# Causal linear attention: values as the stationary operand, four heads in four quarters of columns, divisors from a block of ones

## The chip, the cores and the metric

The kernel runs on one core of a Trainium2 chip. The metric is the device time of one execution in microseconds (us). Three runs of the kernel before took 4279.67, 4286.88 and 4288.96 us; the median is 4286.88 us.

A core has four engines that compute, each with its own queue of instructions that it works off in order: TensorE (PE in the profile; its weight loads are PEld), VectorE (DVE), ScalarE (ACT) and GpSimd (POOL). SyncE (SP) issues the transfers (DMA). TensorE reads its operands from SBUF and writes results to PSUM; VectorE and ScalarE carry results from PSUM to SBUF.

## The reference

The input is 16 sequences of 256 tokens with 128 features. Four layers follow one another, each with a residual and a layer norm: linear attention with four heads, a mixture of eight experts, causal linear attention with 16 heads, and a block of six layers of windowed attention and feed-forward. The change is in the third of them. Cut to what matters:

```python
q = _heads(x @ Wq); k = _heads(x @ Wk); v = _heads(x @ Wv)   # 16 heads of 64
qf = _feature_map(q, Kq)      # softmax(f) and softmax(-f): 128 features
kf = _feature_map(k, Kk)
kv = jnp.cumsum(kf[:, :, :, None, :] * v[..., None], axis=2)
o = jnp.einsum('bhlf,bhldf->bhld', qf, kv)
z = jnp.einsum('bhlf,bhlf->bhl', qf, jnp.cumsum(kf, axis=2)) + EPS
o = o / z[..., None]
y = o.transpose(0, 2, 1, 3).reshape(x.shape[0], x.shape[1], H * HD)
return y @ Wo
```

So for every head and token, the values of all earlier tokens are summed with weights (the inner product of the query's and the key's features), and divided by the sum of those weights.

## The kernel before, in words

**Two stages.** The first holds linear attention (`linear`), experts (`experts`) and causal attention (`causal`); the second holds the six layers. Each stage has a list of steps. A step (class `Step`) belongs to one engine and issues a few instructions; it carries an expected cost in us, the steps it must follow, the buffers it takes, and a rank. `Plan.run` plays these steps through at their expected costs and always issues, on each engine, the ready step of the lowest rank whose buffers are free. The order in which it issues them is the order of the engine's queue on the chip. A wrong cost doesn't make a result wrong; it makes the order fit something else than the chip does. Ranks are offset by the two tables `due` (lines 371 to 399).

**Units.** The first stage works on eight units of two sequences each, that is four tiles of 128 tokens. For each unit `causal` (L761) transposes the stream, calls `part` (L803) four times (two sequences, two halves of eight heads), then `output` (L940) for every tile of 128 tokens, and normalizes.

**In `part`.** Values are computed token-major for eight heads (L817) and copied by ScalarE into the buffer `va` (L820), where each head has 64 columns and a 65th that is always 1.0 (it is set once, L445). Queries and keys go through the feature map: product (L829), largest and smallest of each head (L838, L839), differences on GpSimd (L842, L843), exp on ScalarE (L846), sums and reciprocals on VectorE (L850, L851), a division on GpSimd (L855), a clamp on VectorE (L858), transposes on TensorE (L874), a copy by ScalarE into `fT` (L880). Then come two groups of four heads. For each head:

- `scores` (L893, L894): keys' features times queries' features give the weights in one PSUM bank, with the key tokens as partitions: block 0 is tile 0 against itself, block 1 is keys of tile 0 against queries of tile 1, block 2 is tile 1 against itself.
- `diagonal` (L900, VectorE) masks blocks 0 and 2 with a triangle on the way into the buffer `A`; `below_it` (L906, ScalarE) copies block 1.
- `weigh` (L910 to L912): three matmuls with a block of `A` as the stationary operand and the 65 columns of `va` as the moving one. The result is token-major: 64 weighted sums, and in the 65th column the divisor. It lands in the buffer `two` (tile `pw`, two PSUM banks), of which there is one.

After the four heads `ratio` (L926, L927, L929, VectorE) adds 1e-12 to the divisors, takes their reciprocals, and multiplies the sums by them on the way into `y`, which is token-major and has one buffer per stage.

**In `output`.** Eight transposes of `y` (L951), two copies by ScalarE into `yT` (L954), eight matmuls with `W.o` that add up over the heads' features (L961), and an addition to the stream (L967).

**Weights.** SyncE issues all loads from one queue. `W.o` comes in one transfer (L429), with the heads' features in their natural order over eight blocks of 128 partitions.

Of the kernel before, what the change touches and what calls it, by code (L numbers as in the profile page):

```python
# [16 lines left out]
P = 128  # L17
# [182 lines left out]
def tile_kernel(ctx: ExitStack, tc: tile.TileContext, a: dict, out: bass.AP):  # L200
# [147 lines left out]
    with ExitStack() as st:  # L348
# [5 lines left out]
        def several(pl, n, shape, name):  # L354
# [7 lines left out]
            "h": several(wa, 4, [P, 384], "b_h"),  # L362
            "x": several(wa, 5, [P, 512], "bc_x"),
            "e": several(wa, 4, [P, 8, 2, DH], "c_e"),
            "va": several(wa, 3, [P, TPS, 8, DH + 1], "c_va"),
            "fT": several(wa, 10, [P, 4, SEQ], "c_fT"),
            "y": several(wa, 1, [P, TPS, HEADS, DH], "c_y"),
            "yT": several(wa, 1, [P, 8, P], "c_yT"),
            "A": several(wa, 4, [P, 3, P], "c_A"),
        }  # L370
        plan = Plan(slots, {
            "part.turn": 1.5,
# [29 lines left out]
        def keep_in(shape, src, name):  # L402
            return load(wa, shape, src, name)
# [22 lines left out]

        def weights_c():
            W.v = keep_in([P, INNER], a["L1_attn_Wv"], "c_wv")
            W.o = keep_in([P, 8, P], a["L1_attn_Wo"].rearrange("(c p) d -> p c d", p=P), "c_wo")  # L429
            W.tri = keep_in([P, 3 * P], a["c_tri"], "c_tri")  # L430

        def weights_d():
# [9 lines left out]
        wlb = step("sp", 6.0, weights_b, [wla], rank=-97)  # L442
        wlc = step("sp", 4.0, weights_c, [wlb], rank=-95)
        W.f = {nm: wa.tile([P, INNER], F32, name=f"c_wf{nm}", tag=f"c_wf{nm}") for nm in "qk"}
        for va in slots["va"]:  # L445
            pool.memset(va[:, :, :, DH : DH + 1], 1.0)

        def at(u, j):

# [311 lines left out]
        def causal(u, after, ready, done):  # L761
            rank = 4 * u + due["causal"]
            px, xT, r4 = Buf("bank"), Buf("x"), Buf("x")

            def turn():
                for j in range(TPU):
                    pe.transpose(px.t[:, j * P : (j + 1) * P], at(u, j), ident)

            tn = step("pe", 0.5, turn, [after], [px], [], rank, count=8)
            xc = copied(xT, None, px, 512, [tn], [xT], [], rank, 0.59)  # L770
            ends = []
            for s in range(SPU):
                y = Buf("y")
                ys = []
                for hh in range(2):
                    part(u, s, hh, rank + 2 * s + hh, xT, xc, ready, done, y, ys)
                for t in range(TPS):
                    ends.append(output(u, s, t, rank + 2 * s + 1.5, y, ys, r4, ends))
            nm = norm(
                "c", lambda j: r4.t[:, j * P : (j + 1) * P],  # L780
                lambda j: r4.t[:, j * P : (j + 1) * P], ends, [], [r4], rank + 4,
            )

            def save():
                sp.dma_start(out=keep[u], in_=r4.t)
# [12 lines left out]
            pz = Buf("bank")  # L798
            step("sp", 2.0, save, [nm], [], [r4], rank + 4)
            fn = step("pe", 0.5, partial(final, pz), [nm], [pz], [r4], rank + 4, count=8)  # L800
            step("act", 1.2, partial(stream, pz), [fn], [], [pz], rank + 4)

        def part(u, s, hh, rank, xT, xc, ready, done, y, ys):  # L803
# [8 lines left out]
            for t in range(TPS):  # L812
# [4 lines left out]
                    pe.matmul(pv.t, lhsT=xT.t[:, xj], rhs=W.v[:, c5], start=True, stop=True)  # L817

                def put_v(pv=pv, t=t):
                    act.copy(va.t[:, t, :, 0:DH], pv.t.rearrange("p (h d) -> p h d", d=DH))  # L820

                vm = step("pe", 0.9, values, [xc, wlc, gate, *vs], [pv] + ([] if t else [va]), [xT], rank + due["values"], count=4)
                vs.append(step("act", 0.6, put_v, [vm], [], [pv, va], rank))
# [59 lines left out]
                        fs_done[g].append(step("act", 0.6, put_f, [tn], [], [pz, f], rank))  # L883
            for g in range(2):
                po = Buf("two")
                last, pre = None, None
                for k in range(4):
                    pA, A = Buf("bank"), Buf("A")
                    hl = 4 * g + k

                    def scores(pA=pA, g=g, k=k):
                        qf, kf = fT["q", g].t[:, k, :], fT["k", g].t[:, k, :]
                        pe.matmul(pA.t[:, 0:SEQ], lhsT=kf[:, 0:P], rhs=qf, start=True, stop=True)  # L893
                        pe.matmul(  # L894
                            pA.t[:, SEQ : SEQ + P], lhsT=kf[:, P:SEQ], rhs=qf[:, P:SEQ],
                            start=True, stop=True,
                        )

                    def diagonal(pA=pA, A=A):
                        dve.tensor_tensor(  # L900
                            A.t[:, 0::2, :], pA.t[:, : 3 * P].rearrange("p (b n) -> p b n", n=P)[:, 0::2, :],
                            W.tri.rearrange("p (b n) -> p b n", n=P)[:, 0::2, :], ALU.mult,
                        )

                    def below_it(pA=pA, A=A):
                        act.copy(A.t[:, 1, :], pA.t[:, P : 2 * P])  # L906

                    def weigh(A=A, po=po, k=k, hl=hl):
                        c = slice(k * (DH + 1), (k + 1) * (DH + 1))
                        pe.matmul(po.t[:, 0, c], lhsT=A.t[:, 0, :], rhs=va.t[:, 0, hl, :], start=True, stop=True)  # L910
                        pe.matmul(po.t[:, 1, c], lhsT=A.t[:, 1, :], rhs=va.t[:, 0, hl, :], start=True, stop=False)
                        pe.matmul(po.t[:, 1, c], lhsT=A.t[:, 2, :], rhs=va.t[:, 1, hl, :], start=False, stop=True)  # L912

                    sc = step("pe", 0.66, scores, [*fs_done[g], pre], [pA, A], [fT["q", g], fT["k", g]], rank + due["scores"], count=8)
                    dg = step("dve", 0.45, diagonal, [sc], [], [pA, A], rank + due["diagonal"])
                    bl = step("act", 0.35, below_it, [sc], [], [pA, A], rank + due["diagonal"])
                    last = step(
                        "pe", 0.7, weigh, [dg, bl, *vs, last], [] if k else [po], [A, va] + ([po] if k else []),
                        rank + due["weigh"], count=12,
                    )  # L920
                    pre = sc

                def ratio(po=po, g=g):
                    o4 = po.t[:, :, : 4 * (DH + 1)].rearrange("p t (k d) -> p t k d", d=DH + 1)
                    z = sa.tile([P, TPS, 4], F32, name="c_z")
                    dve.tensor_scalar(z, o4[:, :, :, DH], FEPS, None, ALU.add)  # L926
                    dve.reciprocal(z, z)  # L927
                    h0 = 8 * hh + 4 * g
                    dve.tensor_tensor(  # L929
                        y.t[:, :, h0 : h0 + 4, :], o4[:, :, :, 0:DH], bc(z, [P, TPS, 4, DH], 3),  # L930
                        ALU.mult,
                    )

                first = not ys
                ys.append(
                    step("dve", 1.05, ratio, [last, *ys], [y] if first else [], [po] + ([] if first else [y]), rank + due["ratio"])
                )
            done.append(ys[-1])

        def output(u, s, t, rank, y, ys, r4, ends):  # L940
            j = s * TPS + t
            yT, pr = Buf("yT"), Buf("bank")
            cs = []
            for hf in range(2):
                pz = Buf("bank")

                def turn(pz=pz, hf=hf):
                    yt = y.t[:, t, :, :].rearrange("p h d -> p (h d)")
                    for k in range(4):
                        c = 4 * hf + k  # L950
                        pe.transpose(pz.t[:, k * P : (k + 1) * P], yt[:, c * P : (c + 1) * P], ident)  # L951

                def put(pz=pz, hf=hf):
                    act.copy(yT.t[:, 4 * hf : 4 * hf + 4, :].rearrange("p c n -> p (c n)"), pz.t)  # L954

                tn = step("pe", 0.5, turn, [*ys, *cs], [pz] + ([] if hf else [yT]), [y], rank + due["y"], count=8)
                cs.append(step("act", 0.6, put, [tn], [], [pz, yT], rank))

            def product():
                for c in range(8):  # L960
                    pe.matmul(  # L961
                        pr.t[:, :P], lhsT=yT.t[:, c, :], rhs=W.o[:, c, :],
                        start=(c == 0), stop=(c == 7),
                    )

            def add():
                dve.tensor_tensor(r4.t[:, j * P : (j + 1) * P], pr.t[:, :P], at(u, j), ALU.add)  # L967

            pm = step("pe", 1.86, product, cs, [pr], [yT], rank + due["y"], count=32)
            return step("dve", 0.3, add, [pm, *ends[-1:]], [] if ends else [r4], [pr] + ([r4] if ends else []), rank)  # L970

        ready = [*fused("q"), *fused("k")]
# [703 lines left out]
```

## Time and profile before

| | us |
|---|---|
| median of three runs | 4286.88 (4279.67 to 4288.96) |
| the profiled execution's own time | 4283.78 |
| its span, first to last instruction | 4281.5 |
| PE busy, whole span | 4026.8 (94%) |
| DVE busy, whole span | 3540.7 (83%) |
| ACT busy, whole span | 3147.6 (74%) |
| POOL busy, whole span | 2692.0 (63%) |
| last causal result stored (end of the first stage) | about 1097 |

How to read the lines that follow. A line of the groups names the source line, the engine, the operation, what it writes and reads, the shape and the count; after the bar stand the busy time in us, the mean duration of one instruction in ns, and the time that the engine sat idle just before these instructions, with what ended the idleness. A matmul of 32-bit numbers leaves two records (a transpose one), and records on PE overlap: what a matmul costs in a busy stretch is the distance from its start to the start of the next. `128*128` on PE is the part of the array that is used, rows by columns, so `64*32` is a tile of 64 rows and 32 columns. Lines of the timeline give start and duration in us and the number of records. Lines of stretches give busy time of each engine with the number of its instructions, the granted clock of PE, and the transfers' share. In the waits, "A <- B: 17.9, 9, 3.4" says that A's engine sat idle for 17.9 us in all, nine times, at most 3.4 us, until B was done.

### The profile page before, as it was taken

Reading aid. Unit: us, or ns where it says so; the run is one execution under the profiler, and the core shown is the slowest. Engines: PE = TensorE matmul, PEld = TensorE weight load, DVE = VectorE, ACT = ScalarE, POOL = GpSimd, SP = SyncE. Lnnn points to the kernel's source line nnn. Section 1 sums busy time; section 2 is a strip of 40 time slices with the busy share of each in tenths; the row PEclk is TensorE's granted clock in tenths of the full one; section 3 lists DMA queues with packets and bytes.
Section 4 is the critical chain, followed back from the end, with each engine's and each line's share of the span. In section 5 each row is a group of like instructions: output and inputs, shape, how many; then the busy total and the mean of one; then the engine's idle time right before and its main releaser. Section 6 shows DMA issues by size and latency. Waiting matters only on the chain.

```text
span 4281.5 us, 104658 instructions
## 1 busy us (share of the span) xinstructions
PE 4026.8 (94%) x43728; PEld 2666.5 (62%) x43728; DVE 3540.7 (83%) x5201; ACT 3147.6 (74%) x6106; POOL 2692.0 (63%) x2865
## 2 busy tenths in 40 slices
PE   8999999999799999999999999999999999999888
PEld 5777777787455555565565565565555565555555
DVE  6888888787688888888888888888888888888886
ACT  6766766665478778787778777778787787777675
POOL 2654555566676676667666666766666666766662
PEclk9999999999899999999999999999999999999999
DMA  3000000000000000000000000000000000000000
GB/s 89 4 6 6 4 1 4 3 4 3 20 2 11 2 13 2 7 12 2 13 2 7 11 2 13 2 7 12 2 13 2 7 12 2 2 2 4 9 7 25
DMA packets 30836, 37.03 MB, mean 9 GB/s; under 512 B 5406, under 2 KB 24348, under 8 KB 29596
## 3 DMA queue, kind: packets, MB, share of 16 engines
q1 hardware_dynamic: 30364, 30.35, 2.4%
q8 instruction: 343, 5.62, 0.6%
q14 instruction: 129, 1.06, 0.1%
HBM read 26.15 MB, written 4.19 MB: 7 GB/s over the span
## 4 chain that ended last, share of the span: by engine, by line
PE 54%; DVE 25%; POOL 9%; ACT 8%; issue 4%; SPq 0%; DMA 0%; ACTq 0%; POOLq 0%; DVEq 0%
PE pp L1086 10%; PE pp L1341 8%; PE pp L1160 6%; DVE d_t L1093 5%; DVE d_t L1100 5%; PE pp L1402 4%; ACT d_sq L1107 4%; PE pp L1293 4%; DVE d_e L1242 3%; POOL d_e L1279 3%; PE pp L1234 3%; POOL d_t L1110 2%; PE pp L1422 2%; PE pb L665 2%; DVE d_eT L1283 2%
## 5 line engine op out<-in xcount | busy, mean ns | idle before, releaser
L1110 POOL TENSOR_TENSOR d_t<-d_t,d_t 128x1024 f32<-128x1024 f32 x384 | 904.4, 2360 | 770.0 <-DVE d_t L1093 734.1
L1268 ACT ACTIVATE d_e<-d_e,d_m,d_ny 128x64 f32<-128x64 f32 x3072 | 1071.3, 433 | 90.6 <-POOL d_m L1264 90.0
L1086 PE MATMUL pp<-d_wqkv,xs 128*128 128x512 f32 x1536 | 731.8, 609 | 12.5 <-DVE d_e L1242 6.7
L1341 PE MATMUL pp<-d_zT,d_wvo 128*128 128x256 f32 x3072 | 685.7, 381 | 7.5 <-DVE d_t L1093 2.8
L1100 DVE TENSOR_TENSOR d_t<-pp,d_tab 128x1024 f32<-128x1024 f32 x384 | 467.4, 1218 | 220.6 <-ACT d_sq L1107 126.9
L1341 PEld LDWEIGHTS pp<-d_zT,d_wvo 128*128 128x128 f32 x3072 | 577.8, 191 | 89.5 <-ACT d_sq L1107 8.6
L1107 ACT ACTIVATE d_sq<-pp 128x1024 f32<-128x1024 f32 x384 | 389.0, 1022 | 313.6 <-DVE d_t L1093 102.8
L1302 ACT COPY d_zT<-pp 128x1024 f32<-128x1024 f32 x384 | 373.2, 1012 | 235.1 <-PE pp L1293 235.1
L1093 DVE TENSOR_TENSOR d_t<-pp,d_tab 128x1024 f32<-128x1024 f32 x384 | 465.4, 1213 | 61.7 <-ACT d_sq L1107 61.6
L1113 DVE TENSOR_REDUCE d_ss<-d_sq 128x16 f32<-128x1024 f32 x384 | 455.0, 1201 | 6.4 <-ACT d_sq L1107 5.2
L1293 PE MATMUL pp<-d_eT,d_xw 32*128 32x512 f32 x3072 | 434.1, 618 | 26.2 <-ACT f_xn L1396 17.2
L1160 PE MATMUL pp<-ident,d_t 128*128 128x128 f32 x3072 | 409.4, 280 | 49.3 <-DVE d_t L1093 30.7
L1086 PEld LDWEIGHTS pp<-d_wqkv,xs 128*128 128x128 f32 x1536 | 276.2, 192 | 272.5 <-issue 225.2
L1234 PEld LDWEIGHTS pp<-d_kT,d_qT 64*32 64x32 f32 x24576 | 238.6, 106 | 329.8 <-issue 296.1
L1160 PEld LDWEIGHTS pp<-ident,d_t 128*128 128x128 f32 x3072 | 340.9, 143 | 144.2 <-issue 57.7
L1279 POOL TENSOR_TENSOR d_e<-d_e,d_z 128x1024 f32<-128x1024 f32 x192 | 365.1, 1902 | 46.5 <-DVE d_z L1276 43.0
L1156 POOL TENSOR_TENSOR d_t<-d_t,d_ny 128x1024 f32<-128x1024 f32 x192 | 363.2, 1903 | 0.4
L855 POOL TENSOR_TENSOR c_e<-c_e,c_sm 128x1024 f32<-128x1024 f32 x128 | 248.7, 1950 | 178.1 <-DVE c_sm L851 125.0
L1234 PE MATMUL pp<-d_kT,d_qT 64*32 64x64 f32 x24576 | 333.6, 224 | 8.0 <-ACT d_kT L1166 4.5
L1283 DVE STREAM_TRANSPOSE d_eT<-d_e 128x1024 f32<-128x1024 f32 x192 | 237.6, 1238 | 105.3 <-POOL d_e L1279 105.2
L1402 PE MATMUL pp<-f_xn,d_w 128*128 128x512 f32 (+1 forms) x576 | 276.5, 605 | 29.5 <-DVE d_e L1242 27.8
L1293 PEld LDWEIGHTS pp<-d_eT,d_xw 32*128 32x128 f32 x3072 | 156.4, 184 | 186.8 <-issue 87.8
(184 smaller groups left out, 7252.5 us busy)
## 6 DMA issues: line engine op xcount, KB each, us to landing
d_wqkv<-L_ffn_Wqkv SPq DMA_DIRECT2D x6, 1024.0 KB
d_t<-L_ffn_Wqkv SPq DMA_DIRECT2D x10, 256.0 KB
d_t<-L_ffn_Wo SPq DMA_DIRECT2D x10, 256.0 KB, 3.5
a_xin<-L_attn_x SPq DMA_DIRECT2D x8, 256.0 KB, 2.9
keep<-bc_x SPq DMA_DIRECT2D x8, 256.0 KB, 2.0
d_t<-keep SPq DMA_DIRECT2D x8, 256.0 KB, 3.9
out<-d_t SPq DMA_DIRECT2D x8, 256.0 KB, 2.3
d_w<-L_ffn_W SPq DMA_DIRECT2D x6, 341.0 KB
```

The source lines that it names most:

```text
L1086: pe.matmul(pj.t[:, hf * 512 : (hf + 1) * 512], lhsT=xj, rhs=q.w["qkv"][:, c : c + 512], start=True, stop=True,)
L1093: dve.tensor_tensor(t1.t, heads(pj.t), bc(q.lay.tab[:, 0, t, cc], hs, 1), ALU.mult)
L1100: dve.tensor_tensor(t2.t.rearrange("p h (x d) -> p h x d", x=2), swapped(pj.t), bc(q.lay.tab[:, 1, t, cc].rearrange("p (x d) -> p x d", x= ...
L1107: act.activation(sq.t, heads(pj.t), AF.Square)
L1110: pool.tensor_tensor(t1.t, t1.t, t2.t, ALU.add)
L1113: dve.tensor_reduce(q.ss.t[:, t, qk, :], sq.t, AX.X, ALU.add)
L1160: pe.transpose(pz.t[:, c * P : (c + 1) * P], t1.t[:, 2 * c : 2 * c + 2, :].rearrange("p h d -> p (h d)"), ident,)
L1234: pe.matmul(pS.t[b * WIN : (b + 1) * WIN, s0 : s0 + 2 * WIN], lhsT=qT.t[r, c, b * WIN : (b + 1) * WIN], rhs=kT.t[r, c, k0 : k0 + 2 * WIN], ...
L1268: act.activation(each()[:, h, :], each()[:, h, :], AF.Exp, bias=o.m[:, h : h + 1], scale=norm_of(h),)
L1279: pool.tensor_tensor(each(), each(), bc(o.z, es, 2), ALU.mult)
L1293: pe.matmul(ps[b // 2].t[:, (b % 2) * 512 : (b % 2 + 1) * 512], lhsT=q.xw.t[r, 2 * t + j, :], rhs=eT.t[r, j, :, :].rearrange("p h n -> p ( ...
L1341: pe.matmul(pr.t[:, :SEQ], lhsT=q.w["vo"][:, (h % 2) * 8 + h // 2, :], rhs=q.zT.t[:, :, h, :], start=(h == 0), stop=(h == HEADS - 1),)
```

## The change

The weighted sum is turned round. The values are now the stationary operand and the weights `A` the moving one, so that the result comes out feature-major, as the product with `W.o` needs it.

- A group's four heads stand in four quarters of the PSUM partitions (32 each). A matmul takes 32 of a head's 64 features at a time (128 rows by 32 columns of the array): half 0, half 1, and instead of the 65th column a block `ones` of 128 by 32, whose result is the divisor, repeated on 32 partitions. These are three steps per group (`x` = 2, 0, 1), each with eight matmuls: four of 256 columns (blocks 0 and 1 at once, keys of tile 0) and four of 128 (block 2).
- All four heads' `A` must be ready before a group's first sum, so there are six `A` buffers instead of four; the scores now follow one another over all groups (`chain`).
- `ratio` works feature-major: the addition and the reciprocal on 128x256, the multiplication on 128x512. The buffer `y` is gone; `ratio` writes into `yT`, which has one buffer for a whole sequence.
- The transposes of `y` and the copies into `yT` are gone from `output`.
- `W.o` is loaded in eight transfers, in the order of features that the quarters give.
- The 65th column of `va` and the three memsets for it are gone.

```diff
-            "va": several(wa, 3, [P, TPS, 8, DH + 1], "c_va"),
+            "va": several(wa, 3, [P, TPS, 8, DH], "c_va"),
-            "y": several(wa, 1, [P, TPS, HEADS, DH], "c_y"),
-            "yT": several(wa, 1, [P, 8, P], "c_yT"),
-            "A": several(wa, 4, [P, 3, P], "c_A"),
+            "yT": several(wa, 1, [P, 8, SEQ], "c_yT"),
+            "A": several(wa, 6, [P, 3, P], "c_A"),
...
-            W.o = keep_in([P, 8, P], a["L1_attn_Wo"].rearrange("(c p) d -> p c d", p=P), "c_wo")
+            W.o = wa.tile([P, 8, P], F32, name="c_wo", tag="c_wo")
+            wo = a["L1_attn_Wo"].rearrange("(g k x f) d -> k x f g d", k=4, x=2, f=32)
+            for k in range(4):
+                for x in range(2):
+                    sp.dma_start(out=W.o[k * 32 : (k + 1) * 32, x::2, :], in_=wo[k, x])
...
-                    def weigh(A=A, po=po, k=k, hl=hl):
-                        c = slice(k * (DH + 1), (k + 1) * (DH + 1))
-                        pe.matmul(po.t[:, 0, c], lhsT=A.t[:, 0, :], rhs=va.t[:, 0, hl, :], start=True, stop=True)
-                        pe.matmul(po.t[:, 1, c], lhsT=A.t[:, 1, :], rhs=va.t[:, 0, hl, :], start=True, stop=False)
-                        pe.matmul(po.t[:, 1, c], lhsT=A.t[:, 2, :], rhs=va.t[:, 1, hl, :], start=False, stop=True)
...
+                def weigh(x, As=As, po=po, g=g):
+
+                    o = po.t[:, x // 2, (x % 2) * SEQ : (x % 2 + 1) * SEQ]
+                    f = slice(x * 32, (x + 1) * 32)
+                    for t in range(TPS):
+                        for k in range(4):
+                            lhsT = ones if x == 2 else va.t[:, t, 4 * g + k, f]
+                            rhs = As[k].t[:, 2, :] if t else As[k].t[:, 0:2, :].rearrange("p b n -> p (b n)")
+                            pe.matmul(
+                                o[k * 32 : (k + 1) * 32, t * P :], lhsT=lhsT, rhs=rhs,
+                                start=(t == 0), stop=(t == TPS - 1),
+                            )
+
+                last = None
+                for x in (2, 0, 1):
+                    first = last is None
                     last = step(
-                        "pe", 0.7, weigh, [dg, bl, *vs, last], [] if k else [po], [A, va] + ([po] if k else []),
-                        rank + due["weigh"], count=12,
-                    )
+                        "pe", 0.8, partial(weigh, x), [*cut, *vs, last], [po] if first else [],
+                        [*As, va] + ([] if first else [po]), rank + due["weigh"], count=32,
+                    )
...
                 def ratio(po=po, g=g):
-                    z = sa.tile([P, TPS, 4], F32, name="c_z")
-                    dve.tensor_scalar(z, o4[:, :, :, DH], FEPS, None, ALU.add)
+                    z = sa.tile([P, SEQ], F32, name="c_z", bufs=1)
+                    c = 2 * (2 * hh + g)
+                    dve.tensor_scalar(z, po.t[:, 1, 0:SEQ], FEPS, None, ALU.add)
                     dve.reciprocal(z, z)
                     dve.tensor_tensor(
-                        y.t[:, :, h0 : h0 + 4, :], o4[:, :, :, 0:DH], bc(z, [P, TPS, 4, DH], 3),
-                        ALU.mult,
+                        y.t[:, c : c + 2, :], po.t[:, 0, :].rearrange("p (x n) -> p x n", x=2),
+                        bc(z, [P, 2, SEQ], 1), ALU.mult,
                     )
...
-                    step("dve", 1.05, ratio, [last, *ys], [y] if first else [], [po] + ([] if first else [y]), rank + due["ratio"])
+                    step("dve", 1.3, ratio, [last, *ys], [y] if first else [], [po] + ([] if first else [y]), rank + due["ratio"])
...
-                tn = step("pe", 0.5, turn, [*ys, *cs], [pz] + ([] if hf else [yT]), [y], rank + due["y"], count=8)
-                cs.append(step("act", 0.6, put, [tn], [], [pz, yT], rank))
...
-            pm = step("pe", 1.86, product, cs, [pr], [yT], rank + due["y"], count=32)
+            pm = step("pe", 1.86, product, ys, [pr], [y], rank + due["y"], count=32)
```

More of the change, by code (lines that the diff above doesn't have):

```diff
@@ L444, in tile_kernel @@
         W.f = {nm: wa.tile([P, INNER], F32, name=f"c_wf{nm}", tag=f"c_wf{nm}") for nm in "qk"}
-        for va in slots["va"]:
-            pool.memset(va[:, :, :, DH : DH + 1], 1.0)
+        ones = wa.tile([P, 32], F32, name="c_ones", tag="c_ones")
+        pool.memset(ones, 1.0)
+        chain = []
         def at(u, j):
@@ L772, in causal @@
             for s in range(SPU):
-                y = Buf("y")
+                y = Buf("yT")
                 ys = []
@@ L819, in put_v @@
                 def put_v(pv=pv, t=t):
-                    act.copy(va.t[:, t, :, 0:DH], pv.t.rearrange("p (h d) -> p h d", d=DH))
+                    act.copy(va.t[:, t, :, :], pv.t.rearrange("p (h d) -> p h d", d=DH))
                 vm = step("pe", 0.9, values, [xc, wlc, gate, *vs], [pv] + ([] if t else [va]), [xT], rank + due["values"], count=4)
@@ L885, in part @@
                 po = Buf("two")
-                last, pre = None, None
+                cut = []
+                As = []
                 for k in range(4):
                     pA, A = Buf("bank"), Buf("A")
-                    hl = 4 * g + k
                     def scores(pA=pA, g=g, k=k):
@@ L914, in part @@
-                    sc = step("pe", 0.66, scores, [*fs_done[g], pre], [pA, A], [fT["q", g], fT["k", g]], rank + due["scores"], count=8)
-                    dg = step("dve", 0.45, diagonal, [sc], [], [pA, A], rank + due["diagonal"])
-                    bl = step("act", 0.35, below_it, [sc], [], [pA, A], rank + due["diagonal"])
+                    sc = step("pe", 0.66, scores, [*fs_done[g], *chain[-1:]], [pA, A], [fT["q", g], fT["k", g]], rank + due["scores"], count=8)
+                    chain.append(sc)
@@ new lines, in part @@
+                    As.append(A)
+                    cut.append(step("dve", 0.45, diagonal, [sc], [], [pA, A], rank + due["diagonal"]))
+                    cut.append(step("act", 0.35, below_it, [sc], [], [pA, A], rank + due["diagonal"]))
+                def weigh(x, As=As, po=po, g=g):
[9 more added lines that the diff above has]
+                            )
@@ L920, in part @@
                     )
-                    pre = sc
                 def ratio(po=po, g=g):
-                    o4 = po.t[:, :, : 4 * (DH + 1)].rearrange("p t (k d) -> p t k d", d=DH + 1)
-                    z = sa.tile([P, TPS, 4], F32, name="c_z")
-                    dve.tensor_scalar(z, o4[:, :, :, DH], FEPS, None, ALU.add)
+                    z = sa.tile([P, SEQ], F32, name="c_z", bufs=1)
+                    c = 2 * (2 * hh + g)
+                    dve.tensor_scalar(z, po.t[:, 1, 0:SEQ], FEPS, None, ALU.add)
@@ L927, in ratio @@
                     dve.reciprocal(z, z)
-                    h0 = 8 * hh + 4 * g
                     dve.tensor_tensor(
-                        y.t[:, :, h0 : h0 + 4, :], o4[:, :, :, 0:DH], bc(z, [P, TPS, 4, DH], 3),
-                        ALU.mult,
+                        y.t[:, c : c + 2, :], po.t[:, 0, :].rearrange("p (x n) -> p x n", x=2),
+                        bc(z, [P, 2, SEQ], 1), ALU.mult,
                     )
@@ L941, in output @@
             j = s * TPS + t
[L942 to L954, printed above, removed]
-                tn = step("pe", 0.5, turn, [*ys, *cs], [pz] + ([] if hf else [yT]), [y], rank + due["y"], count=8)
-                cs.append(step("act", 0.6, put, [tn], [], [pz, yT], rank))
+            pr = Buf("bank")
             def product():
@@ L961, in product @@
                     pe.matmul(
-                        pr.t[:, :P], lhsT=yT.t[:, c, :], rhs=W.o[:, c, :],
+                        pr.t[:, :P], lhsT=y.t[:, c, t * P : (t + 1) * P], rhs=W.o[:, c, :],
                         start=(c == 0), stop=(c == 7),
```

## The prediction

> **What bounds the kernel now.** I read the page first: PE is busy 94% of the span, and the diff touches only the first of two stages (linear attention, experts, causal attention). On every engine the changed program's instruction order is the old one again from the second stage on. So the question is about some 1100 us out of 4281.5, and stretches of that stage come next:
>
> ```profile
> core 0: us, PE busy (x) PEld busy (x) DVE busy (x) ACT busy (x) POOL busy (x), PEclk, DMA share, GB/s
> 100.00:400.00 300.00, 286.45 (x1811) 231.81 (x1810) 255.22 (x571) 205.51 (x422) 167.99 (x124) 0.98 0.01 5
> 400.00:700.00 300.00, 287.77 (x1829) 235.40 (x1827) 249.33 (x546) 200.72 (x414) 154.62 (x117) 0.98 0.01 4
> 700.00:900.00 200.00, 194.20 (x1251) 158.46 (x1249) 164.27 (x356) 135.75 (x282) 118.00 (x86) 1.00 0.01 2
> 900.00:1097.00 197.00, 181.12 (x1167) 152.25 (x1165) 140.41 (x294) 109.03 (x218) 100.96 (x75) 0.95 0.01 4
> sum 997.00, PE 949.54 PEld 777.91 DVE 809.22 ACT 651.02 POOL 541.57; mean PE 237.38 PEld 194.48 DVE 202.31 ACT 162.75 POOL 135.39
> ```
>
> The reader is to see that PE is busy 95% of the stage, but DVE is second with 81%. Added up from 100 to 1095 us, the chain of work that ended last lies 600 us on PE, 240 on DVE, 72 on POOL and 67 on ACT: 60%, 24%, 7%, 7%. PE leads, with DVE close. The groups that the change touches, from the stage's list of groups:
>
> ```profile
> L910 PE MATMUL pw<-c_va,c_A 128*128 128x65 f32 x512 | 91.5, 261 | 26.6 <-DVE c_y L929 17.9 <-DVE c_A L900 8.1
> L929 DVE TENSOR_TENSOR c_y<-pw,c_z 128x512 f32<-128x512 f32 x64 | 44.2, 691 | 2.2
> L951 PE MATMUL pb<-ident,c_y 128*128 128x128 f32 x256 | 38.4, 273 | 0.6 <-DVE c_y L929 0.6
> L954 ACT COPY c_yT<-pb 128x512 f32<-128x512 f32 x64 | 38.1, 597 | 8.7 <-PE pb L951 6.5 <-issue 2.2
> L851 DVE RECIPROCAL c_sm<-c_sm 128x16 f32<-128x16 f32 x128 | 32.4, 253 | 4.4
> L927 DVE RECIPROCAL c_z<-c_z 128x8 f32<-128x8 f32 x64 | 13.0, 203 | 2.2
> L926 DVE TENSOR_SCALAR c_z<-pw 128x8 f32<-128x8 f32 x64 | 9.8, 154 | 26.1 <-PE pw L912 25.6
> L900 DVE TENSOR_TENSOR c_A<-pb,c_tri 128x256 f32<-128x256 f32 x256 | 100.6, 407 | 23.0 <-ACT c_A L906 14.0 <-PE pb L894 7.5
> ```
>
> Here the two reciprocals matter: twice the elements, 50 ns more.
>
> **PE, what goes.** Matmuls overlap, so I count from start to start in the timeline of PE:
>
> ```profile
> 317.51 0.33 PE L910 MATMUL pw<-c_va,c_A 128*128 128x65 f32 x2
> 317.69 0.39 PE L911 MATMUL pw<-c_va,c_A 128*128 128x65 f32 x2
> 317.91 0.39 PE L912 MATMUL pw<-c_va,c_A 128*128 128x65 f32 x2
> 318.13 0.86 PE L665 MATMUL pb<-b_w,bc_x 128*128 128x384 f32 x2
> 318.83 0.59 PE L893 MATMUL pb<-c_fT,c_fT 128*128 128x256 f32 x2
> 319.26 0.38 PE L894 MATMUL pb<-c_fT,c_fT 128*128 128x128 f32 x2
> 319.48 0.33 PE L910 MATMUL pw<-c_va,c_A 128*128 128x65 f32 x2
> ```
>
> One head's three weighted sums take 0.62 us (317.51 to 318.13); there are 64 groups of four heads, so 256 x 0.62 = 158.7 us go. The transposes of y go too: four of them start within 0.44 us in the timeline, 0.11 each, 256 x 0.11 = 28 us.
>
> **PE, what comes.** 192 steps (64 groups, three x), each with four matmuls of 256 columns and four of 128. If the four quarters of columns run beside each other, a step costs one matmul of each size: 0.65 us, the scores pair from 318.83 to 319.48. Whether they run beside each other, and what a change of form costs, the second stage shows:
>
> ```profile
> 1172.28 0.46 PE L1234 MATMUL pp<-d_kT,d_qT 64*32 64x64 f32 x32 [4.32 <-ACT d_kT L1166]
> 1172.67 1.70 PE L1160 MATMUL pp<-ident,d_t 128*128 128x128 f32 x8
> 1177.82 3.70 PE L1086 MATMUL pp<-d_wqkv,xs 128*128 128x512 f32 x8
> 1181.45 1.17 PE L1234 MATMUL pp<-d_kT,d_qT 64*32 64x64 f32 x96
> ```
>
> L1234 uses eight tiles of 64 rows by 32 columns: 96 records in 1.17 us. At the rate of the rows above (0.215 us a record of 256 columns) a 64-column record is 0.054 us of one tile, so 96 in a row would be 5.2 us, and two row tiles alone 2.6. Its first eight records start 7 ns apart. So quarters of columns do run together. A 32-column weight load is left uncovered between first and second pass (0.08 us instead of 0.054), some 0.03 a step. The changed form is entered and left: equal forms overlap by 0.16 us (318.83 + 0.59 against 319.26), unequal ones by 0.07 (1177.82 + 3.70 against 1181.45; 1172.28 + 0.46 against 1172.67). Each change of form costs 0.09 us. In the changed program's PE order the 192 steps form 185 runs between matmuls of the full form, so 370 changes, 33 us. Sum: 192 x 0.68 + 33 = 164 us. The weighted sums are thus no cheaper (164 for 158.7); with the transposes PE is relieved of **23 us**.
> The Trainium skill, "TensorE: Matmul & The Clock Gate", section "Measured speedup vs the span model", gives 2.38 times for three column tiles, where three would be full. An estimate by it puts 0.82 us for 0.65, so 33 us more on PE, which would end its relief; no row here has 128 rows by 32 columns, and the L1234 row speaks for the full rate.
>
> **DVE.** The ratio has the same three operations 64 times, but divisors come as 128x256, one for each of 32 feature rows, instead of 128x8. Multiplication keeps its 512 elements: 0.69. The addition reads 256 elements from PSUM: L900 does as many in 0.41, against 0.154. The reciprocal has no such row. Lower end: one element at the addition's slope, (407 - 154)/248 = 1.02 ns, so 0.253 + 240 x 1.02 ns = 0.50 us. Upper end: the slope between this stage's two-element reciprocal (155 ns, L563) and L927, 8 ns an element: 0.253 + 240 x 8 ns = 2.17 us. I take the slope between L927 and L851, the nearest pair: 50 ns / 8 = 6.25 ns, 0.253 + 240 x 6.25 ns = **1.75 us**. The ratio is then 0.41 + 1.75 + 0.69 = 2.85 us against 1.05: 64 x 1.80 = **+115 us** (ends: +36 and +142). The planner in the kernel is told 1.3 us, so it sets the order as if 1.55 us of each ratio weren't there; diagonals (L900), gated products and clamps queue behind it on DVE, and weighted sums, hidden transposes and feature transposes wait for those.
> The Trainium skill, "VectorE: DVE Perf Modes", section "First, the fixed hardware budget", has the reciprocal as an iterated divide with a repeat count of 8; at that page's 0.96 GHz an estimate is 8.3 ns an element, +147 us. The two rows give 6.25, and I go by them.
>
> **ACT and the rest.** 64 copies of 0.597 us go from ACT: -38 us, on an engine with 7% of the chain: -3 us. POOL loses three memsets. SP issues eight DMAs for W.o instead of one: 7 x 0.43 us (its issue rows) = 3 us for loads queued behind, the mask, x of unit 2, the second stage's weights. The first product with W.o starts at 169.5 us and the load is issued at 18.4, so this is nothing; without that cover it would be 3 us. y now holds its one buffer through the product, where it was freed at the transposes; the product is 8 matmuls, 1.8 us, in 16 places, and two copies of 0.6 us vanish ahead of it: nothing net.
>
> **The new wait.** pw has one buffer: the next group's first sum waits for the ratio, with all of PE queued behind it.
>
> ```profile
> PE pw L910 <- DVE c_y L929: 17.9, 9, 3.4
> ```
>
> With the weight loads it is 27 us in 20 places. In the old order 27 of 63 neighbours have only 1.9 to 2.8 us of PE work between one group's last sum and the next one's first; as the ratio itself is 1.05, some 1.9 us go to latency and to DVE's queue. In the new order 33 have less than 6.6 us. Needing 1.9 + 2.85 = 4.75 us, the shortfalls add up to 30 us. So this wait costs about what it did: +3 us.
>
> **Sum.** In the stage's 1000 us DVE goes from 812 to 927, PE from 953 to 930. Break-even needs both engines busy 93% at once, each in a fixed order that leaves 1.55 us of every ratio out. I price by the chain: DVE's share is 24% now and would be about half of the two's 84% when they're level, so 33% on average: 0.33 x 115 = +38. PE's falls from 60% to 42%: 0.51 x -23 = -12. With -3 for ACT and +3 for pw that is +26 us. The profiled execution took 4283.8 us, 2.3 around its span and 3.1 below the median of the runs: 4283.8 + 26 = **4310 us**, slower.
>
> **Rivals.**
> 1. The reciprocal is fast (0.50 us). DVE gains 36 us: 0.25 x 36 - 0.58 x 23 - 3 = -7, up to -23 if PE alone decides: 4261 to 4277, faster. For it: large operands may stream. Against it: 50 ns for 8 elements. It decides from below about 2 ns an element. 14%.
> 2. The reciprocal is slow but DVE's idle 188 us absorb it, and the stage follows PE: -23 us, 4261. Against it: DVE idles because it waits for PE, ACT and POOL (c_mx for ACT 31 us, c_z for PE 26). 8%. With half of it absorbed the time is level (4275 to 4292): 12%.
> 3. DVE becomes the plain bound at 8 ns an element: 812 + 142 = 954 us at 88% busy, the mean of what PE (95%) and DVE (81%) reach now: 1084, +84, with a queue that holds up pw, up to 4400. 13%.
> 4. Quarters of columns don't run together. Two at a time: 192 x 0.65 = +125, 4409; one at a time: 192 x 1.95 = +374, near 4660. 5%.
>
> **How the numbers follow.** My forecast, 4293 to 4345, has 48%. About 0.2%, 8.6 us, can be told from no change. Faster: 11 of rival 1 and 8 of rival 2, 19%. Same: 3 and 12, 15%. Slower: 48, 13 and 5, 66%. The range from 4262 to 4385 leaves out rival 4, the end of 3 and the edge of the fast cases.
>
> **What would show it.** c_z's reciprocal at 1.5 to 2.2 us; DVE above 90% of the stage and a larger part of its chain; a weighted-sum step at 0.65 to 0.7 us with 0.09 at each edge; PE idle time released by c_yT and c_A grown; the second stage equal to 1%. The forecast is wrong if the reciprocal is under 0.6 us, or if PE stays at 95% of a shorter stage.

## The result, and the profile after

The changed kernel takes 4314.9 us (median of four runs, 4309.2 to 4316.8); the kernel before, run beside it, takes 4285.3. The ratio is 1.0067, with an interval of 1.0052 to 1.0082: **slower, by about 29 us**. The forecast was 4310 us, slower.

The second stage starts (first product of L1087) at 1126.7 us in the profiled execution, where the old kernel starts it at 1097.9: 28.8 us later. From there to the end it is 3180.7 us against 3183.6. So in the profiled executions (4309.2 and 4283.8 us, 25.4 apart) the whole difference lies in the first stage, as the prediction had it. The same stretches as before (columns: length, then busy time and count of PE, PEld, DVE, ACT and POOL, granted clock, DMA):

```profile
100.00:400.00 300.00, 279.42 (x2117) 193.43 (x2116) 272.54 (x552) 192.37 (x389) 161.88 (x120) 0.98 0.02 5
400.00:700.00 300.00, 287.82 (x2193) 200.92 (x2192) 269.20 (x543) 195.67 (x402) 154.57 (x116) 0.99 0.01 4
700.00:900.00 200.00, 188.49 (x1453) 130.56 (x1452) 175.88 (x342) 127.22 (x259) 105.31 (x77) 1.00 0.01 2
900.00:1122.00 222.00, 190.48 (x1569) 133.21 (x1568) 183.47 (x321) 110.52 (x222) 115.10 (x87) 0.98 0.01 3
sum 1022.00, PE 946.21 PEld 658.12 DVE 901.09 ACT 625.76 POOL 536.85; mean PE 236.55 PEld 164.53 DVE 225.27 ACT 156.44 POOL 134.21
```

PE's busy time hardly moves (949.5 to 946.2) in a stage that got longer; DVE's rises from 809 to 901. The groups of the ratio, of the clamp and of the weighted sums, from the list of groups of the first 1122 us:

```profile
L863 DVE TENSOR_SCALAR c_e<-c_e 128x1024 f32<-128x1024 f32 x128 | 121.4, 962 | 2.0 <-POOL c_e L860 1.9
L944 DVE RECIPROCAL c_z<-c_z 128x256 f32<-128x256 f32 x64 | 112.2, 1753 | 2.2
L945 DVE TENSOR_TENSOR c_yT<-pw,c_z 128x512 f32<-128x512 f32 x64 | 44.2, 691 | 2.2
L943 DVE TENSOR_SCALAR c_z<-pw 128x256 f32<-128x256 f32 x64 | 25.8, 403 | 20.2 <-PE pw L927 19.9
L927 PE MATMUL pw<-c_A,c_ones 128*32 128x256 f32 x512 | 55.9, 404 | 17.1 <-DVE c_yT L945 14.5 <-DVE c_A L905 1.6 <-ACT c_A L911 1.0
```

The reciprocal of 256 elements takes 1753 ns, the three operations together 2.85 us, both as worked out. And one step of sums in PE's timeline:

```profile
417.86 0.86 PE L927 MATMUL pw<-c_A,c_ones 128*32 128x256 f32 x16
418.64 0.94 PE L699 MATMUL pb<-b_w,b_h 128*128 128x128 f32 x6
419.51 0.86 PE L927 MATMUL pw<-c_A,c_va 128*32 128x256 f32 x16
420.30 0.91 PE L670 MATMUL pb<-b_w,bc_x 128*128 128x384 f32 x2
```

From start to start a step is 0.78 to 0.79 us. That contains the change of form behind it, that is the change from 32 columns back to the full array: the modelled 0.86 us overlap the next matmul by 0.070 us, where equal forms overlap by 0.163, so a change costs 0.093. The step alone is 0.695 us, with a change at both ends 0.88.

**Where the 29 us are.** I split the time from 100 us to the start of the second stage by PE's records: *idle* is every gap behind the modelled end of a matmul, plus the 0.163 us by which equal neighbours overlap (a stall eats that first); *half clock* is half of the time in which PE's granted clock was 0.5; *work* is the rest. Worked out from the records of each trace (how a gap is counted where two records touch moves idle and work by up to 3 us; e7 is left out):

| kernel | stage until, us | idle | half clock | work |
|---|---|---|---|---|
| before | 1097.9 | 56.7 | 22.2 | 919.1 |
| after | 1126.7 | 95.2 | 15.2 | 916.2 |
| e1: after, no reciprocal | 1059.2 | 46.3 | 4.8 | 908.2 |
| e2: before, with long reciprocal | 1181.4 | 111.7 | 50.8 | 919.0 |
| e3: after, two reciprocals | 1264.6 | 186.4 | 61.2 | 916.9 |
| e4: after, ratio planned at 2.85 | 1107.8 | 87.2 | 8.8 | 911.8 |
| e5: after, reciprocal last | 1124.2 | 89.2 | 14.0 | 921.0 |
| e6: after, three sums in one step | 1091.3 | 96.2 | 14.2 | 880.9 |
| e8: e6, ratio planned at 2.85 | 1119.5 | 121.7 | 16.7 | 881.1 |
| e9: after, ratio planned at 2.0 | 1097.3 | 73.1 | 13.2 | 911.0 |
| e10: before, ratio planned at 1.3 | 1077.2 | 48.9 | 8.4 | 919.9 |
| e11: e9, no reciprocal | 1063.9 | 48.3 | 7.2 | 908.5 |
| e12: e6, ratio planned at 2.0 | 1113.5 | 110.2 | 20.7 | 882.6 |

PE's work is the same within 1.5% for each form (before, three steps, one step). What differs is how long PE stands idle and what it loses at half clock. From before to after: idle +38.5, half clock -7.0, work -2.9.

### The profile page after: what moved, and what is told of

It reads as the page before. It is cut to its first block, busy times and chain, and to the rows that moved or that the text cites. A ratio compares the mean times of both kernels' runs of the same rounds, so it can differ in the third digit from the quotient of the medians.

```text
span 4307.4 us, 107164 instructions
## 1 busy us (share of the span) xinstructions
PE 4020.7 (93%) x45008; PEld 2545.5 (59%) x45008; DVE 3635.0 (84%) x5201; ACT 3123.5 (73%) x6043; POOL 2691.7 (62%) x2863
## 3 DMA queue, kind: packets, MB, share of 16 engines
q14 instruction: 130, 1.06, 0.1%
## 4 chain that ended last, share of the span: by engine, by line
PE 39%; DVE 19%; POOL 7%; ACT 6%; issue 4%; ACTq 0%; DVEq 0%; POOLq 0%
PE pp L1087 10%; PE pp L1342 9%; PE pp L1161 6%; DVE d_t L1094 5%; DVE d_t L1101 5%; PE pp L1403 4%; PE pp L1294 4%; ACT d_sq L1108 4%; DVE d_e L1243 3%; PE pp L1235 3%; POOL d_e L1280 3%; PE pp L1423 2%; DVE d_eT L1284 2%; POOL d_t L1111 2%; DVE d_m L1257 1%
## 5 line engine op out<-in xcount | busy, mean ns | idle before, releaser
L1087 PE MATMUL pp<-d_wqkv,xs 128*128 128x512 f32 x1536 | 729.6, 607 | 13.2 <-DVE d_e L1243 6.7
L1087 PEld LDWEIGHTS pp<-d_wqkv,xs 128*128 128x128 f32 x1536 | 275.6, 192 | 272.4 <-issue 224.2
```

What stands on the lines that cost most here:

```text
L1087: pe.matmul(pj.t[:, hf * 512 : (hf + 1) * 512], lhsT=xj, rhs=q.w["qkv"][:, c : c + 512], start=True, stop=True,)
```

## The experiments

The theory: the reciprocals load DVE, and PE waits for what DVE hands on late. Rivals: the wait for pw does it (e5), the planned order does it (e4, e9, e10), or the weighted sums' new form does it (e6). The kernel before took 4281.6 to 4285.9 us beside the several experiments, so times from different experiments compare to some 4 us; each ratio is to the kernel before that ran beside it.

### What the reciprocals cost: e1, e2, e3

**e1_no_recip** leaves the reciprocal out (the output is multiplied by the divisor instead of its inverse), and has the instruction order of the changed kernel:

```diff
                     dve.tensor_scalar(z, po.t[:, 1, 0:SEQ], FEPS, None, ALU.add)
-                    dve.reciprocal(z, z)
```

> The changed kernel without the 64 reciprocals on 128x256 (the sums are multiplied by the divisors themselves, so the division is left out); costs told to the planner, and so the order on every engine, as in the changed kernel. Theory (VectorE's 112 us of reciprocals are what the change costs): the relief on TensorE and ScalarE is left alone, -12 and -3 us by the chain's shares against the kernel before, some 4265 to 4275 us, about 45 us below the changed kernel. Rival (the changes of form and the single pw buffer cost it): no more than 15 us below the changed kernel, 4300 or above.

Measured: 4246.6 us, ratio to before 0.9916 (0.9901 to 0.9931), below both expectations. The reciprocals cost 68 us of their 112 us in this order, and all the rest of the change *gains* 36 (against 4282.7 for the kernel before beside this run, hence 68 - 36 and not quite 29). PE's waits of the first stage (who waits, for what: sum, times, longest), before, after and then e1:

```profile
PE pb L874 <- DVE c_e L858: 8.0, 5, 3.0
```

```profile
PE pb L879 <- DVE c_e L863: 20.1, 14, 2.4
PE pw L927 <- DVE c_yT L945: 14.5, 10, 3.1
```

```profile
PE pb L879 <- DVE c_e L863: 13.4, 15, 3.0
PE pw L927 <- DVE c_yT L944: 2.9, 3, 1.4
```

The first line of each is the feature transposes' wait for the clamp, which stands in the same DVE queue as the ratios: 8.0 us in before, 20.1 in after. Without the reciprocals both these transposes and the next group's sums (pw) wait less.

**e2_before_slow** adds a reciprocal of 256 elements to each ratio of the kernel *before*; its result is overwritten:

```diff
+                    dve.reciprocal(
+                        y.t[:, 0, h0 : h0 + 4, :], W.f["q"][:, 0:SEQ].rearrange("p (h d) -> p h d", d=DH)
+                    )
                     dve.tensor_tensor(
```

> The kernel before, with one reciprocal of 256 elements (1.75 us, result overwritten afterwards) put into each ratio ahead of its multiplication; the order on every engine stays that of before. VectorE alone gets the change's load, TensorE and ScalarE stay as they were. Theory: a third of 112 us shows, +37 us, 4315 to 4330 us. Rival (VectorE's idle 188 us of the stage absorb it): within 10 us of before, 4277 to 4295.

Measured: 4367.0 us, 1.0197 (1.0181 to 1.0212): +84 us for 109 us of added DVE work, with nothing else of the change. Theory had a third of it, the rival none. The load alone is enough for a loss, and in this order at three quarters of its length. PE's largest wait:

```profile
PE pw L910 <- DVE c_y L932: 60.8, 32, 5.0
```

These waits have an aftermath. PE's timeline, and the stretches (columns as above) around one of them:

```profile
196.12 0.69 PE L910 MATMUL pw<-c_va,c_A 128*128 128x65 f32 x2 [1.67 <-DVE c_y L932]
196.60 0.64 PE L911 MATMUL pw<-c_va,c_A 128*128 128x65 f32 x2
197.03 0.63 PE L912 MATMUL pw<-c_va,c_A 128*128 128x65 f32 x2
197.46 1.82 PE L621 MATMUL pb<-b_gw,bc_x 128*128 128x8 f32 x8
```

```profile
188.90:195.80 6.90, 5.26 (x25) 3.23 (x23) 6.80 (x16) 4.64 (x11) 1.90 (x1) 1.00 0.00 1
195.80:209.40 13.60, 13.28 (x52) 11.43 (x53) 11.59 (x25) 4.79 (x8) 2.12 (x1) 0.50 0.00 1
209.40:216.20 6.80, 6.80 (x43) 5.15 (x42) 2.82 (x5) 4.95 (x10) 1.90 (x2) 1.00 0.01 2
```

DVE is full (6.80 of 6.90), and PE waits 1.67 us for it, until 196.12. From 195.80, still within that wait, the granted clock is 0.50 for 13.6 us: the three sums take 1.34 us (196.12 to 197.46) where the prediction's rows had 0.62. PE is busy for 13.3 of these 13.6 us, so an estimate is that a wait of 1.7 us was followed by another 6.6 us lost. In the whole stage 102 us are at half clock, in before 44.

**e3_double_recip** does the reciprocal twice in the changed kernel; the second result is overwritten:

```diff
                     dve.reciprocal(z, z)
+                    dve.reciprocal(y.t[:, c, :], z)
```

> The changed kernel with a second reciprocal of 256 elements per ratio (result overwritten afterwards): the dose doubled, order unchanged. Theory: VectorE's share of the chain grows with its load, so the second 112 us cost more than the first, 60 to 100 us: 4375 to 4415 us. Rival (the stage is bound by TensorE and its waits): less than 30 us more, below 4345.

Measured: 4445.5 us, 1.0378 (1.036 to 1.0395), above both expectations. The second dose costs 130 us, more than it lasts (112); in the profiled execution, 8 us above the median, idle time grows by 91 and half clock by 46. So there is no single price for DVE's time: the same 112 us cost 68 as a first dose, and 130 as a second.

### Load or wait: e5

**e5_late_recip** divides afterwards: the multiplication frees pw, and the reciprocal comes behind it (outputs are multiplied by the divisor, whose inverse nothing uses). DVE's load is the same, and pw is free 1.75 us sooner:

```diff
-                    dve.reciprocal(z, z)
                     dve.tensor_tensor(
                         y.t[:, c : c + 2, :], po.t[:, 0, :].rearrange("p (x n) -> p x n", x=2),
                         bc(z, [P, 2, SEQ], 1), ALU.mult,
                     )
+                    dve.reciprocal(z, z)
```

> The changed kernel with the reciprocal moved behind the multiplication in each ratio (the sums are multiplied by the divisors themselves, so the division is left out, but the reciprocal still runs): VectorE has the changed kernel's whole load in the same order, and only pw comes free 1.75 us earlier. Theory (VectorE's load delays everything behind it; the waits on clamps, masks and feature extremes carry it): 4290 to 4312 us, the larger part of the 68 us that the reciprocals cost stays. Rival (the one pw buffer is what turns the reciprocal into lost time): 4247 to 4270 us, as without reciprocals.

Measured: 4305.6 us, 1.0055 (1.004 to 1.007): within the theory's range, and 9 us less than after (5 by the ratios), hardly resolved (the two intervals overlap; the first stage of the profiled execution is 2.5 us shorter). What replaces the wait for pw, which falls from 14.5 to 2.9 us:

```profile
PE pb L879 <- DVE c_e L863: 19.8, 13, 3.0
PE pw L927 <- DVE c_A L905: 9.2, 12, 1.4
```

The transposes wait for the clamp as they did, and the sums now wait for the diagonals (L905, in after 1.6 us), which stand behind the reciprocal in DVE's queue. So in this order it is the load, not the buffer. A second buffer for pw or for yT wasn't tried.

### The order of the planner: e4, e9, e10, e11

The changed kernel tells the planner 1.3 us for a ratio that takes 2.85. **e4_cost_285** and **e9_cost_20** change only that number, **e10_before_cost13** gives the old kernel 1.3 in place of 1.05, and **e11_no_recip_20** is e9 without reciprocals (the division is left out, as in e1). The edit of e4; with 2.0 that of e9 and e11, and from 1.05 to 1.3 that of e10:

```diff
-                    step("dve", 1.3, ratio, [last, *ys], [y] if first else [], [po] + ([] if first else [y]), rank + due["ratio"])
+                    step("dve", 2.85, ratio, [last, *ys], [y] if first else [], [po] + ([] if first else [y]), rank + due["ratio"])
```

> The changed kernel with the planner told the ratio's real 2.85 us instead of 1.3: the same work in another order. Theory (the load itself costs): 0 to -12 us, 4303 to 4315 us. Rival (the wrong cost in the plan makes the loss, the load would fit): most of the 30 us come back, 4275 to 4292 us.

> The changed kernel with the planner told 2.0 us for the ratio, half way from 1.3 to the real 2.85. If the true cost helps because the order makes room for VectorE, the gain grows with the cost told: between the two, 4300 to 4310 us. If the 22 us at 2.85 were the luck of one order among many, this may fall anywhere, above 4315 too.

> The kernel before with the planner told 1.3 us for the ratio, as the changed kernel tells it (real: 1.05): the same work in another order. It measures how far the choice of an order alone moves the kernel before. If its own order is of the usual kind: within 10 us, 4275 to 4295. If orders scatter as widely as in the changed kernel (4283 to 4315): anything from 4270 to 4310.

> The changed kernel without reciprocals (the division is left out) in the order of the planned cost of 2.0 us, whose time with reciprocals is 4283. If the reciprocals' 68 us hold in any order: about 4215 us. If the order made at 2.0 us simply hides more of VectorE's load: 4235 to 4255 us, a price of 30 to 45 us.

Measured: e4 4293.3 us, 1.0027 (1.0017 to 1.0037); e9 4283.1, 0.9997 (0.9988 to 1.0006); e10 4264.4, 0.9951 (0.9936 to 0.9966); e11 4249.7, 0.9918 (0.9902 to 0.9935). e4 lies between its two expectations, e9 far below the range of its first one, e10 below both of its ranges, and e11 is as its second one had it. The true cost is better than 1.3, but a wrong one between them is better still, and a wrong one helps the old kernel by 21 us. Nothing but the order differs, so an order is worth 10 to 16 us either way. From these five draws it looks as if a planned cost draws another order more than it improves it. The reciprocals cost e9 only 33 us (4283.1 less 4249.7) where they cost after 68; without them both orders take the same (4246.6 and 4249.7). In e10 the waits for the ratio fell in sum:

```profile
PE pw L910 <- DVE c_y L929: 11.2, 11, 2.1
```

The old order had 17.9 us there, and longest 3.4; half clock fell from 22 to 8. Costs beyond these were not tried.

### Relief of PE: e6, e8, e12

**e6_one_step** puts a group's three sums into one step, so that they follow one another and the form changes twice per group at most, not six times:

```diff
-                for x in (2, 0, 1):
-                    first = last is None
-                    last = step(
-                        "pe", 0.8, partial(weigh, x), [*cut, *vs, last], [po] if first else [],
-                        [*As, va] + ([] if first else [po]), rank + due["weigh"], count=32,
-                    )
+                last = step("pe", 2.1, weigh, [*cut, *vs], [po], [*As, va], rank + due["weigh"], count=96)
```

(`weigh` then loops over x itself.)

> The changed kernel with a group's three sums in one step of 24 matmuls (planned at 2.1 us, once 3 x 0.8): 64 runs of the 32-column form instead of 185, so 242 changes of form fewer, 242 x 0.093 = 22.5 us of TensorE. Theory (TensorE still sets the end between VectorE's holds): two thirds of it or more show, 4290 to 4302 us. Rival (VectorE is the bound, TensorE's time is hidden): within 8 us of the changed kernel, 4305 or above.

Measured: 4277.9 us, 0.999 (0.998 to 0.9999): 37 us less than after (33 by the ratios), more than the theory asked for. PE's timeline of one group:

```profile
412.49 0.86 PE L931 MATMUL pw<-c_A,c_ones 128*32 128x256 f32 x16
413.16 1.48 PE L931 MATMUL pw<-c_A,c_va 128*32 128x256 f32 x32
414.57 0.91 PE L670 MATMUL pb<-b_w,bc_x 128*128 128x384 f32 x2
```

The group takes 2.08 us with the change behind it, and 2.17 with the one ahead of it too; three lone steps take 3 x 0.88 = 2.64. 64 x 0.47 = 30 us, and the accounting has 35 us less work at the same idle time. **e8_one_step_285** plans e6 at 2.85 us for the ratio and 2.5 for the sums, **e12_one_step_20** at 2.0 for the ratio:

> The changed kernel with a group's three sums in one step (as in the run with one step) and the planner told 2.85 us for the ratio and 2.5 for the sums. If the two gains (37 us of the one step, 22 of the true cost) come from different waits they add: 4255 to 4262 us. If both remove the same waits: 4270 to 4280 us, as with one step alone.

> The changed kernel with the three sums in one step (planned 2.1 us) and the planner told 2.0 us for the ratio, the cost at which the three-step version was quickest. If the one step's 30 us of TensorE show in any order: 4250 to 4270 us. If orders scatter by 15 us and more around a common level: 4270 to 4300 us.

Measured: e8 4306.2 us, 1.0052 (1.0039 to 1.0064); e12 4297.5, 1.0029 (1.0019 to 1.0039). Neither expectation of e8 held, and e12 gained nothing over e6. PE's work stays low (881 and 883 us), but idle time rises to 122 and 110. So against the three-step kernels with the same cost told for the ratio, one step made things 13 us slower (e8 and e4; e8 also tells another cost for the sums) and 14 us slower (e12 and e9). Less work on PE was a gain in one order and no gain in two others; between e6, e8 and e12 themselves lie 20 to 28 us by the order alone.

### The reciprocal on another engine: e7

**e7_pool_pow** moves the reciprocal to GpSimd, as a power of -1, in a step of its own (planned at 2.0 us) between two on DVE:

```diff
...
+                    pool.tensor_tensor(o.z, o.z, minus.to_broadcast([P, SEQ]), ALU.pow)
...
-                    dve.reciprocal(z, z)
```

> The changed kernel with the reciprocal taken by GpSimd as a power of -1 on 128x256 (planned at 2.0 us, a step of its own between VectorE's addition and multiplication). VectorE loses 112 us. What the power costs on 256 elements no run shows (128x4 takes 1.03 us). Theory: at up to 2.5 us GpSimd goes from 54% to 70% of the stage and the time to 4255 to 4285 us. Rival (GpSimd's power is far slower per element, 10 us or more, and becomes the bound with pw held all the while): above 4400 us.

Measured: 6805 us, 1.589 (1.587 to 1.592); the rival was right. The group on POOL:

```profile
L949 POOL TENSOR_TENSOR c_z<-c_z,c_minus 128x256 f32<-128x256 f32 x64 | 2640.1, 41251 | 144.2 <-DVE c_z L946 144.2
```

41 us for each, 0.16 us an element. The power that both kernels have on POOL (L228, exponent -0.5) is of four elements and takes 1.0 to 1.1 us, and from that its price per element can't be read.

## Why the prediction was right, and where its steps were not

The forecast of +26 us met +29, with the sign, the stage and the load that causes it right. That the number came so near is luck: it is a sum of terms whose errors cancel.

- **The durations: right.** Reciprocal 1.75 us (measured 1.753), ratio 2.85 (2.85), a step of sums 0.68 (0.695), a change of form 0.09 (0.093). The slope of 6.25 ns an element from the rows of 8 and 16 held up to 256. The estimate of 8.3 ns worked out from the Trainium skill ("VectorE: DVE Perf Modes", "First, the fixed hardware budget") would have given 2.2 us; the trace's 1.75 is some 20% below it.
- **Quarters of columns run beside each other: right.** Four matmuls of 256 columns start 7 ns apart. Rival 4 is out. The Trainium skill's 2.38 for three column tiles ("TensorE: Matmul & The Clock Gate", "Measured speedup vs the span model") would make a step 0.82 us, not 0.695; it does not hold for this form here.
- **The wait for pw, put at +3: not dearer, rather less.** PE's own wait is 14.5 us where the old kernel had 17.9, and that of the weight loads 8.3 where it had 27.1 (the prediction's 27 us in 20 places are the weight loads' alone). e5 shows that freeing pw sooner gains 9 or less.
- **DVE's work: 115 us, right, but its busy time rose by less** (809 to 901, 88% of the stage where "above 90%" was to be seen). The clamp became faster: its mean fell from 1167 ns to 962, 27 us in all. A clamp beside which POOL runs no tensor operation takes 0.68 to 0.70 us; those over 1.2 us (43 of 128 before, 30 after) all overlapped such operations.
- **Where PE waits: in part.** Idle time released by c_yT and c_A was to grow, and it shrank at the sums: 17.9 to 14.5 us for the ratio, 8.1 to 1.6 for the diagonals. What grew is the feature transposes' wait for the clamp, 8.0 to 20.1, which the prediction names in its paragraph on DVE but not among its signs; the rest of the 38 us more of idle time is spread over many short waits.
- **DVE's price, "33% on average: 0.33 x 115 = +38": mis-sized.** The chain's share is no price. In after's order the reciprocals alone cost 68 us (e1), in e9's 33, in before's 84 (e2), and a second dose 130 (e3). In all of these PE's work stays within 1.5%, and the load costs by the idle time that it opens on PE plus the change in half clock; the chain of before shows neither how near the other queued steps are to being late, nor the 22 us at half clock that before already had.
- **PE's price, "0.51 x -23 = -12": the relief mis-sized, the share not settled.** Of the 23 us (19 by the measured step: 158.7 + 28 - 192 x 0.695 - 370 x 0.093) the accounting finds 3 in after, 8 in e9, 11 in e1 and e11 and none in e5. An undisturbed step is not the reason, for at least three quarters of after's lone steps at full clock take 0.79 us with the change behind them; where the other 8 to 19 us went isn't settled. What relief is worth depends on the order: e6 took 30 to 35 us from PE and became 37 faster, but e8 and e12 took as much and became slower than e4 and e9, for idle time took it up (e12 against e9: work -28, idle +37, half clock +7).
- **The rest of the change** was forecast at -12 and gained 36 (e1), 11 in PE's work, 10 in idle time and 17 in half clock. Part of it is the order: compared with e10, the better draw of the old kernel, it gains 18 (15 by the ratios).

So 38 - 12 became 68 - 36. And **the size of the result belongs to this pair of orders**: before has 4264 and 4285 in two orders, after 4315, 4283 and 4293 in three. The best order tried of each form keeps the sign: 4264.4 for the old form, 4283.1 for the new one, 4277.9 with one step. Of the kernels that divide as the reference does, e10 is thus the fastest here, and beats both. That the slowdown comes from the reciprocals is shown (without them the new form takes 4247 to 4250 in two orders, below both orders of the old one, and in e2 such a load alone slows the old form). The changes of form weigh too: without two thirds of them e6 is level with before. How many of the 29 us are the draw of an order is not shown, beyond these few draws.

Rival 2 (DVE's idle time absorbs the load) came true in part: of 112 us after absorbs 44, e9 79. Rival 3 (DVE as the plain bound) is nearer to e3, one dose further on, where the dose costs more than it lasts and DVE is busy 1017 of 1165 us.

## What to carry to other kernels

Where one engine sets the end and a second is nearly as full, the busy shares and the chain give no price for work moved between them. Price load put on the second by the waits that it opens on the first; here a second dose cost nearly twice the first. Work taken from the first was worth its full length in one order and nothing in two others. When a change spreads a small operand over 32 times as many elements, look first for the operation with a steep slope per element: here two rows, 50 ns apart, decided the sign. Where a planner draws the order, vary its costs in both kernels before crediting a change with a per cent.

## What the runs showed of the hardware beyond that

- In a wait of 1.7 us on PE began 13.6 us at half clock (e2). Stretches at half clock cost before 22 us, e2 51 and e3 61 by the accounting. The Trainium skill ("TensorE: Matmul & The Clock Gate", "HAM oscillation — how this bites in real kernels") warns of idle gaps above some 3.4 us; here the clock fell in a gap of half that length, 2 us after one of 0.29, and in after, at 341.9 and 608.1 us, less than 1 us behind single gaps of 1.9.
- A power on GpSimd takes 41.25 us for 128x256 (exponent -1) and 1.06 for 128x4 (exponent -0.5): if the exponent makes no difference, which wasn't tried, the slope and not the start is its cost.
- A clamp of 128x1024 on DVE takes 0.69 us with no tensor operation of GpSimd beside it and up to 2.4 us beside one; some that overlap one stay at 0.69.
- A change between full matmuls and 128x32 tiles costs 0.093 us, by the modelled overlaps.
